# Four hand-overs of a four-layer convolution kernel: the first filter buffer, the last image's stores, layer 2's constants, layer 3's norms

## The chip, the cores and the metric

The kernel runs on one core of one Trainium2 chip, as one program and one launch. The metric is device time in microseconds (us). A core has five engines that run at the same time: TensorE (PE in the profile, its weight loads PEld), VectorE (DVE), ScalarE (ACT), GpSimd (POOL) and SyncE (SP). Each works through its own instructions in order. In this kernel nearly all DMAs are issued from SP's queue, so an SP issue that has to wait holds back every DMA behind it.

## The reference, cut to what matters

The input is 32 images of 96 channels of 56x56 values in float32. Four layers follow one another, each as `x = x + layer(groupnorm(x))`, the group norm in 32 groups of 3 channels:

```
x = x + L0(_gn(x))   # 1x1 96->576, BN, silu; depthwise 3x3, BN, silu; squeeze-excite; 1x1 576->96, BN; + identity
x = x + L1(_gn(x))   # depthwise 5x5 plus a three-level Haar wavelet transform with 5x5 depthwise filters on each level
x = x + L2(_gn(x))   # 4-bit quantised: 1x1 96->576, BN, clip, round; depthwise 3x3, ...; 1x1 576->96, BN; + identity
x = x + L3(_gn(x))   # depthwise 9x9 with a kernel computed from a 2x2 metric of each channel
```

In layer 2 a weight is quantised as `t = tanh(w); t = t / (2 max|t|) + 0.5; 2 round(15 t) / 15 - 1`.

## The kernel before, in words

**Layers 0 and 2** work image by image with channels on the partitions. An order written out by hand (`L0_ORDER`, `L2_ORDER`) fixes the sequence of steps on PE, DVE and ACT; `run_steps` walks it for image after image, with steps of the image before (`-`) and after (`+`) mixed in. In layer 0, `e` expands a block (PE, then ACT evicts into the padded buffer `hpad`, line 308), `f` makes a block's first depthwise tap on ACT (line 316), `t` makes one of the other eight taps on DVE (line 321), `a` and `c` make two further blocks' depthwise on PE (line 344), `p` projects (lines 402 to 405), `d` adds to the image (line 410) and `o` takes the image's statistics and stores it (line 417). The order begins:

```
    e00 e01 e02 e03 z0- f0 a3- z2- c1- e10 e11 t01 t02 g0- e12 t03 e30 e40 g1- s+ e13 t04 g2- g3-
    e31 e32 t05 e33 g4- t06 t07 u+ f1 m+ t11 p0- p1- q+ t08 d0- v+ w+ p2- t12 ...
```

**The tables.** Before layer 0's images, `tables()` makes the filters of layers 1 and 3 in the on-chip memory: `wavelet_filters` on DVE, with three buffers `zt` that POOL clears (line 485) and SP stores as `zwav` (line 497), and `diffusion_filters`, most of it on POOL (two `pow` at lines 1070 and 88, copies into `zdt`, line 1086), stored as `zdiff` (line 1087). All of it lies in one pool, `tables`, which is closed afterwards. The filter buffers `h2` of layer 0 (pool `l0h`, five of them) and the pool `l0l` are then opened where `tables` lay. From the stored filters SP builds matrices in DRAM (`twav`, `tdiff`) during layer 0.

**The end of layer 0.** When the last image is added, SP stores it in six DMAs, one for each group of 16 channels (`y0`, line 417). `store_norm` works out the scale and shift of layer 1's group norm for all channels and images (lines 106 to 119, with a `pow` on POOL at line 114) and SP stores the row (line 120) behind the image.

**Layer 1** works by pairs of channels, with rows of 14 image rows by phase on the partitions. For each pair, SP loads `X` (lines 538 and 541), `raw` and `T` matrices and `nr`, the row of norms (line 583), three pairs ahead; DVE normalises two pairs ahead (lines 654 and 655), ACT and DVE split `x` into two parts (`xh` line 662, `xl` line 666), and PE does the rest. The constants of layer 1 (`low1`, `up1`, `low2`, `up2`, line 604) are loaded first. After each pair, `behind` has SP load finished channel groups of `y1` into layer 2's first two image pairs (line 840).

**Layer 2's constants** are made by `Layer2.__init__` between layers 0 and 1: three weights are loaded (line 782) into a pool of their own, `l2t`, go through `tanh` on ACT (line 783), a largest value (DVE line 785, an all-reduce on POOL line 787) and rounding on DVE (lines 788 to 794); DVE then makes 45 diagonal matrices (line 808), and `folded` makes scales and offsets (lines 818 to 828).

**The end of layer 2** is like that of layer 0, but images are stored two at a time (line 1036). **Layer 3** works channel by channel: `load` first loads, for every eighth channel, the norms of eight channels (line 1107), then `X` and `raw`; ACT arranges `T`, DVE normalises (lines 1118 and 1119), PE filters (line 1126), DVE adds (line 1127), SP stores (line 1142).

Of the kernel before, what the change touches and what calls it, by code (L numbers as in the profile page):

```python
# [10 lines left out]
F32 = mybir.dt.float32  # L11
BF16 = mybir.dt.bfloat16
# [86 lines left out]
def store_norm(nc, S, pool, psum, mv, dram, bias):  # L99


    mc, d, dv, ve = (pool.tile([C, B], F32, tag=f"n{n}", name=f"n{n}", bufs=1) for n in ("mc", "d", "dv", "ve"))
    row = pool.tile([C, 2 * B + 1], F32, tag="row", name="row", bufs=1)
    rstd = row[:, 0:B]
    ps = psum.tile([128, 2, 512], F32, tag="mm", name="pn")
    nc.vector.tensor_copy(mc, mv[:, :, 0])
    nc.tensor.matmul(ps[:C, 0, :B], S.grp, mc, start=True, stop=True)
    nc.vector.tensor_tensor(d, mc, ps[:C, 0, :B], ALU.subtract)
    nc.vector.tensor_tensor(dv, d, d, ALU.mult)
    nc.vector.tensor_tensor(dv, dv, mv[:, :, 1], ALU.add)  # L110
    nc.vector.tensor_tensor(d, mc, d, ALU.subtract)
    nc.tensor.matmul(ps[:C, 1, :B], S.grp, dv, start=True, stop=True)
    nc.vector.tensor_scalar(ve, ps[:C, 1, :B], EPS_GN, None, ALU.add)
    nc.gpsimd.tensor_tensor(rstd, ve, S.mhalf[:C, :B], ALU.pow)
    nc.vector.scalar_tensor_tensor(row[:, B : 2 * B], d, -1.0, rstd, ALU.mult, ALU.mult)
    if bias is None:
        nc.vector.memset(row[:, 2 * B :], 0.0)
    else:
        nc.vector.tensor_copy(row[:, 2 * B :], bias)
    nc.sync.dma_start(dram, row)  # L120
# [24 lines left out]
def groups(t, y, at, store=False):  # L145

    for g in range(C // GR):
        part = t[g * GR : (g + 1) * GR], at(y[g])
        yield part[::-1] if store else part

# [13 lines left out]
def layer0(ctx, tc, S, x, w, y0, norm1, tables, aside):  # L164
# [66 lines left out]
    eye2 = cp.tile([128, HALF], F32, tag="eye2", name="eye2")  # L231
    nc.vector.tensor_tensor(eye2, S.ident[:, :HALF], S.ident[:, HALF:], ALU.add)
    diag = cp.tile([128, 2, 9, HALF], F32, tag="diag", name="diag")
# [3 lines left out]

    hpad = padded(cp, nc, 4, F32, "hpad")
    mv_all = cp.tile([C, B, 2], F32, tag="mv0", name="mv0")


    tables()
    hp = ctx.enter_context(tc.tile_pool(name="l0h", bufs=5))
    late = ctx.enter_context(tc.tile_pool(name="l0l", bufs=1))

# [68 lines left out]
    def first_tap(im, k):  # L314
        im["h2"][k] = hp.tile([128, H, W], F32, tag="h2", name="h2")
        nc.scalar.activation(im["h2"][k], window(im["pad"][k], 128, -1, -1, 0, H), AF.Copy,  # L316
                             scale=wdw[:, k, 0:1])
# [32 lines left out]
    def depthwise_ab(im, i):  # L350
        if i == 0:
            im["hab"] = late.tile([128, NP, 2, NT], F32, tag="hab", name="hab")
# [5 lines left out]
    def depthwise_c(im, i):  # L358

        if i == 0:  # L360
            im["hc"] = late.tile([128, 2, 2, NT], F32, tag="hc", name="hc")
# [28 lines left out]
    def gated(im):  # L390
        im["wg"] = late.tile([128, ND + 1, C], F32, tag="wg", name="wg")
# [15 lines left out]
    def add(im, i):  # L407
        for j in range(2):
            v = tiles(im["xt"])[:, i, j::2]
            nc.vector.scalar_tensor_tensor(  # L410
                v, im["ps"][i][:C, j, :NT].rearrange("c (x m) -> c m x", m=2), sc3, v, ALU.mult, ALU.add)

    def store(im):
        b, xt = im["b"], im["xt"]
        channel_stats(nc, sm, xt, mv_all[:, b, :], "t")
        for to, of in groups(xt, y0, lambda y: y[:, :, b, :], store=True):
            nc.sync.dma_start(to, of)
# [26 lines left out]
def wavelet_filters(nc, cp, w, z1, z2, z3):  # L444
# [15 lines left out]
    for v, z in enumerate((z1, z2, z3)):  # L460
# [23 lines left out]
        Z = cp.tile([C, 2, P, LEN, P, ks], F32, tag=f"z{v}", name=f"zt{v}")  # L484
# [12 lines left out]
        nc.sync.dma_start(z, Z.rearrange("c a p e o k -> c a p (e o k)"))  # L497

# [89 lines left out]
def layer1(ctx, tc, w, y0, norm, t1, t2, t3, y1, behind):  # L588
# [147 lines left out]
    with tc.manual_schedule(engines=MANUAL_SP):  # L736
        for i in range(-3, PAIRS):
# [25 lines left out]
            behind(2 * i + 2)  # L763


class Layer2:


    def __init__(self, ctx, tc, S, w, y1):
# [3 lines left out]
        self.pairs = [cp.tile([C, H * NPH, 2, W4], F32, tag=f"xt{i}", name=f"xt{i}") for i in range(2)]  # L773
        self.begun = 0

        CC, HALF, N9 = NBLK - 1, 64, 2 * NBLK - 1


        def quantized(name, shape, dtype):
            p, free = shape[0], shape[1:]  # L780
            t = tmp.tile(shape, F32, tag="t", name=f"{name}t")
            nc.sync.dma_start(t, w[name])
            nc.scalar.activation(t, t, AF.Tanh)
            m = cp.tile([p, 1], F32, tag=f"{name}m", name=f"{name}m")
            nc.vector.tensor_reduce(m, t, AX.X if len(free) == 1 else AX.XY, ALU.max, apply_absolute_value=True)
            a = cp.tile([p, 1], F32, tag=f"{name}a", name=f"{name}a")
            nc.gpsimd.partition_all_reduce(a, m, p, bass_isa.ReduceOp.max)
            nc.vector.tensor_scalar(a, a, 2.0, None, ALU.mult)
            nc.vector.reciprocal(a, a)
            nc.vector.tensor_scalar(t, t, a, 0.5, ALU.mult, ALU.add)  # L790
            nc.vector.tensor_scalar(t, t, 15.0, MAGIC, ALU.mult, ALU.add)
            nc.vector.tensor_scalar(t, t, MAGIC, 2.0, ALU.subtract, ALU.mult)
            o = cp.tile(shape, dtype, tag=f"{name}q", name=f"{name}q")
            nc.vector.tensor_scalar(o, t, 15.0, None, ALU.subtract)
            return o

        with tc.tile_pool(name="l2t", bufs=3) as tmp:
            w1 = quantized("l2_w1", [C, NBLK * 128], F32R)
            w2 = quantized("l2_w2", [128, NBLK, 9], F32)
            w3 = quantized("l2_w3", [128, N9 + 1, C], BF16)  # L800
        nc.vector.memset(w3[HALF:, N9 - 1, :], 0.0)
        nc.vector.memset(w3[:HALF, N9, :], 0.0)
        eye2 = cp.tile([128, HALF], F32, tag="eye2", name="eye2")
        nc.vector.tensor_tensor(eye2, S.ident[:, :HALF], S.ident[:, HALF:], ALU.add)
        diag = cp.tile([128, NBLK, 9, HALF], BF16, tag="diag2", name="diag2")
        for k in range(NBLK):
# [3 lines left out]
        mid = cp.tile([128, 10, N9], F32, tag="mid2", name="mid2")  # L810
        nc.sync.dma_start(mid, w["l2_mid"])
        out5 = cp.tile([C, 5, 1], F32, tag="out5", name="out5")
        nc.sync.dma_start(out5, w["l2_out"])
        def folded(a, p, n, tag, k, times):

            b_, g, be, m, v = (a[:, i, :] for i in range(5))
            s = cp.tile([p, n], F32, tag=f"s{tag}", name=f"s{tag}")
            nc.gpsimd.tensor_scalar(s, v, EPS_L2, None, ALU.add)
            nc.gpsimd.tensor_tensor(s, s, S.mhalf[:p, :n], ALU.pow)
            nc.vector.tensor_tensor(s, s, g, ALU.mult)  # L820
            o = cp.tile([p, n], F32, tag=f"o{tag}", name=f"o{tag}")
            nc.vector.tensor_tensor(o, b_, m, ALU.subtract)
            nc.vector.tensor_tensor(o, o, s, ALU.mult)
            nc.vector.tensor_tensor(o, o, be, ALU.add)
            if times != 1.0:
                nc.vector.tensor_scalar(o, o, times, None, ALU.mult)
            if k * times != 1.0:
                nc.vector.tensor_scalar(s, s, k * times, None, ALU.mult)
            return s, o

        s1, o1 = folded(mid[:, 0:5, :], 128, N9, "1", 1.0 / 15.0, 15.0)
        s2, o2 = folded(mid[:, 5:10, :], 128, N9, "2", 1.0 / 225.0, 15.0)
        s3, o3 = folded(out5, C, 1, "3", 1.0 / 225.0, 1.0)
        self.constants = w1, w3, diag, s1, o1, s2, o2, s3, o3

# [9 lines left out]
def layer2(ctx, tc, S, k2, y1, y2, norm3):  # L845
# [19 lines left out]
    pairs = k2.pairs + [cp.tile([C, H * NPH, 2, W4], F32, tag="xt2", name="xt2")]  # L865
# [158 lines left out]
    def add(im, i):  # L1024
        for j in range(2):
# [3 lines left out]
                v, im["ps"][i][:C, j, :NT].rearrange("c (r q) -> c r q", q=W4), s3, v, ALU.mult, ALU.add)  # L1029

    def store(im):
        b = im["b"]
        channel_stats(nc, sm, im["xt"], mv_all[:, b, :], "t")
        if b % 2:
# [15 lines left out]
def diffusion_filters(nc, cp, w, zd):  # L1050

# [22 lines left out]
    nc.gpsimd.tensor_tensor(kern, poi, kern, ALU.add)  # L1074
    rev = cp.tile([C, KS, KS], F32, tag="rev", name="rev")
    for ky in range(KS):
        nc.gpsimd.tensor_copy(rev[:, KS - 1 - ky], kern[:, KS * ky : KS * ky + KS])
    Z = cp.tile([C, NPH, LEN, NPH, NK], F32, tag="zd", name="zdt")
# [12 lines left out]
def layer3(ctx, tc, w, y2, norm, td, out):  # L1091
# [11 lines left out]
    def load(c):  # L1103
        if c % NN == 0:
            norms[c] = io.tile([128, NN, 2 * B + 1], F32, tag="nr", name="nr", bufs=3)
            rows = norm[c : c + NN].rearrange("c x -> (c x)").unsqueeze(0)
            nc.sync.dma_start(norms[c].rearrange("p c x -> p (c x)"), rows.to_broadcast([128, NN * (2 * B + 1)]))
        X = io.tile([128, 2, B, W4], F32, tag="X", name="X")
        load_halves(nc, X, y2[c // GR][c % GR])
        return {"X": X, "raw": load_matrices(nc, io, td, c), "nr": norms[c // NN * NN][:, c % NN]}  # L1110
# [18 lines left out]
    with tc.manual_schedule(engines=MANUAL_SP):  # L1129
        for c in range(-AHEAD, C):  # L1130
            if c + AHEAD < C:
                sts[c + AHEAD] = load(c + AHEAD)
            cur, far = sts.pop(c, None), sts.get(c + 2)
            if far:
                far["T"] = arranged(nc, io, far["raw"])
# [10 lines left out]
def kernel_body(tc, w, x, out):  # L1146
    nc = tc.nc
    with ExitStack() as ctx:
# [24 lines left out]
        def tables():  # L1173
            with tc.tile_pool(name="tables", bufs=1) as tp:
                wavelet_filters(nc, tp, w, z1, z2, z3)
                diffusion_filters(nc, tp, w, zd)
# [4 lines left out]
        with ExitStack() as ctx2:  # L1181
            k2 = Layer2(ctx2, tc, S, w, y1)

            layer1(tc, w, y0, norm1, t1, t2, t3, y1, lambda channels: k2.begin(min(channels - 2, C - GR)))
# [124 lines left out]
```

## Time and profile before

| | |
|---|---|
| median of 9 runs | 6487.06 us (6471.28 to 6495.83) |
| the profiled execution: its time, its span | 6489.56 us, 6487.6 us |
| instructions | 115298 |
| PE busy | 6023.1 us, 93% of the span |
| DVE busy | 5168.0 us, 80% |
| ACT busy | 3949.9 us, 61% |
| POOL busy | 206.9 us, 3% |
| mean granted TensorE clock | 0.966 |

The span runs from the first to the last instruction of one profiled execution; the time also has what lies around it, 2.0 us here. Rows of the timeline give start and duration in us, engine, line of the kernel, operation, output and inputs, the number of merged instructions and in brackets the idle time before and what ended it. A row of SPq is the issuing of DMAs, not their transfer.

In the page's 40 slices of 162 us, PE is busy for nine tenths or more of nearly every slice; the exceptions are the first slice, one at the change from layer 0 to layer 1, one at the change from layer 1 to layer 2, and one at the change from layer 2 to layer 3, besides the last.

### The profile page before, as it was taken

Reading aid. Unit: us, or ns where it says so; the run is one execution under the profiler, and the core shown is the slowest. Engines: PE = TensorE matmul, PEld = TensorE weight load, DVE = VectorE, ACT = ScalarE, POOL = GpSimd, SP = SyncE. Lnnn points to the kernel's source line nnn. Section 1 sums busy time; section 2 is a strip of 40 time slices with the busy share of each in tenths; the row PEclk is TensorE's granted clock in tenths of the full one; section 3 lists DMA queues with packets and bytes.
Section 4 is the critical chain, followed back from the end, with each engine's and each line's share of the span. In section 5 each row is a group of like instructions: output and inputs, shape, how many; then the busy total and the mean of one; then the engine's idle time right before and its main releaser. Section 6 shows DMA issues by size and latency. Waiting matters only on the chain. (4 is left out here: it accounts for less than half of the span.)

```text
span 6487.6 us, 115298 instructions
## 1 busy us (share of the span) xinstructions
PE 6023.1 (93%) x49064; PEld 3598.6 (55%) x49064; DVE 5168.0 (80%) x5468; ACT 3949.9 (61%) x5268; POOL 206.9 (3%) x158
## 2 busy tenths in 40 slices
PE   4999999999999999999949999989999999999699
PEld 2444444444444444444426555567777777778344
DVE  6999999998998998989946666657676767676577
ACT  4665666665765755656525555557676766677355
POOL 3000000000000000000010000000000000000000
PEclk7999999999999999999969999999999999999899
DMA  2162264528327264522535666656959595952688
GB/s 82 22 42 45 49 47 40 52 47 36 50 44 38 50 35 48 34 47 37 16 73 139 148 140 142 141 40 40 53 41 52 39 54 38 53 38 27 172 252 250
DMA packets 1609376, 452.91 MB, mean 70 GB/s; under 512 B 1425230, under 2 KB 1603142, under 8 KB 1605406
## 3 DMA queue, kind: packets, MB, share of 16 engines
q1 hardware_dynamic: 1608862, 445.54, 55.5%
q8 instruction: 385, 6.31, 0.5%
q14 instruction: 129, 1.06, 0.1%
HBM read 284.44 MB, written 214.08 MB: 77 GB/s over the span
## 5 line engine op out<-in xcount | busy, mean ns | idle before, releaser
L321 DVE SCALAR_TENSOR_TENSOR h<-hpad,l_wdw,h 128x3136 f32<-128x3136 f32 x768 | 2659.7, 3481 | 56.3 <-ACT h L316 42.3
L344 PE MATMUL psd<-hpad,diag 64*64 64x392 f32 x13824 | 1235.3, 511 | 3.3 <-issue 3.3
L308 ACT ACTIVATE hpad<-ps,o,s 128x784 f32<-128x784 f32 x640 | 684.3, 1080 | 774.4 <-PE ps L304 772.6
L304 PE MATMUL ps<-xn,l_wexp 96*128 96x392 f32 x2560 | 934.1, 517 | 103.0 <-ACT hpad L308 97.3
L984 PE MATMUL psd<-apad,diag 64*64 64x392 bf16 x20736 | 926.9, 332 | 110.3 <-issue 56.1
L344 PEld LDWEIGHTS psd<-hpad,diag 64*64 64x64 f32 x13824 | 528.6, 131 | 699.2 <-issue 660.4
L984 PEld LDWEIGHTS <-diag 64*64 64x64 bf16 x20736 | 712.1, 107 | 321.0 <-issue 161.1
L304 PEld LDWEIGHTS ps<-xn,l_wexp 96*128 96x128 f32 x2560 | 495.0, 198 | 492.6 <-ACT hpad L308 103.3
L955 ACT ACTIVATE u<-ps,o,s 128x784 int16<-128x784 f32 x576 | 536.4, 1002 | 160.5 <-PE ps L965 142.0
L955 ACT ACTIVATE a<-psd,o,s 128x784 int16<-128x784 f32 x448 | 426.8, 997 | 325.9 <-PE psd L984 324.5
L402 PE MATMUL psj<-h,wg 128*96 128x392 f32 x1536 | 589.0, 519 | 27.7 <-ACT hpad L308 26.1
L550 ACT COPY T<-raw 32x112 f32<-32x112 f32 (+2 forms) x1440 | 462.7, 384 | 242.9 <-DMA raw<-tdiff 211.2
L965 PE MATMUL ps<-hi,l_w1q 96*128 96x392 f32 x1280 | 461.5, 361 | 9.9 <-ACT hi L937 9.2
L1126 PE MATMUL pc<-x,T 128*112 128x416 f32 (+1 forms) x1152 | 415.7, 524 | 43.5 <-DMA X<-y 42.7
L721 PE MATMUL pc<-x,T 128*112 128x416 f32 (+1 forms) x1152 | 450.8, 528 | 0.0
L965 PE MATMUL ps<-lo,l_w1q 96*128 96x392 f32 x1280 | 436.8, 341 | 0.0
L402 PEld LDWEIGHTS psj<-h,wg 128*96 128x96 f32 x1536 | 248.8, 165 | 287.5 <-issue 255.9
L1126 PEld LDWEIGHTS pc<-x,T 128*112 128x112 f32 x1152 | 204.6, 178 | 254.0 <-issue 194.2
L327 ACT ACTIVATE hab<-psd,o,s 128x392 f32<-128x392 f32 x256 | 170.7, 671 | 262.3 <-PE psd L344 262.3
L316 ACT ACTIVATE h<-hpad,l_wdw 128x3136 f32<-128x3136 f32 x96 | 279.2, 2908 | 48.2 <-DMA zdiff<-zdt 47.1
L327 ACT ACTIVATE h<-h,o,s 128x3136 f32<-128x3136 f32 x96 | 287.9, 2999 | 18.6 <-DVE h L321 18.6
L721 PEld LDWEIGHTS pc<-x,T 128*112 128x112 f32 x1152 | 193.0, 180 | 146.6 <-issue 146.6
(207 smaller groups left out, 6766.1 us busy)
## 6 DMA issues: line engine op xcount, KB each, us to landing
X<-y SPq DMA_DIRECT2D x192, 392.0 KB
xt<-in_x_dram SPq DMA_DIRECT2D x32, 1176.0 KB
y<-xt SPq DMA_DIRECT2D x192, 196.0 KB
y<-y SPq DMA_DIRECT2D x96, 392.0 KB
xt<-y SPq DMA_DIRECT2D x96, 392.0 KB
y<-xt SPq DMA_DIRECT2D x96, 392.0 KB
out_dram<-y SPq DMA_DIRECT2D x96, 392.0 KB
twav<-zwav SPq DMA_DIRECT2D x768, 36.8 KB
```

The costliest lines, as they stand in the source:

```text
L304: nc.tensor.matmul(ps[:, j, :NT], wexp[:, k * 128 : k * 128 + 128], im["xn"][:, j, rows, :].rearrange("c h w -> c (h w)"), start=True, sto ...
L308: nc.scalar.activation(window(im["pad"][k], 128, 0, 0, 2 * i * RT, 2 * RT).rearrange("p r (w j) -> p j r w", j=2), ps[:, :, :NT].rearrange ...
L321: nc.vector.scalar_tensor_tensor(h2, window(im["pad"][k], 128, t // 3 - 1, t % 3 - 1, 0, H), wdw[:, k, t : t + 1], h2, ALU.mult, ALU.add,)
L327: nc.scalar.activation(view, ps, AF.Silu, bias=bi[1][:, c : c + 1], scale=sc[1][:, c : c + 1], accum_out=accum)
L344: nc.tensor.matmul(ps[c * HALF : (c + 1) * HALF, j, :NT].rearrange("p (r w) -> p r w", w=W2), diag[p, k - AB, t, :], v[:, :, j:W:2], start ...
L402: nc.tensor.matmul(out.rearrange("c (r w) -> c r w", w=W2), wg[:, k, :], im["h2"][k][:, rows, j::2], start=(k == 0), stop=False)
L550: nc.scalar.copy(to.rearrange("x t (p s) -> x t p s", p=NPH), v[:, k])
L721: nc.tensor.matmul(ps[:PH, to], st["T"][j][:, h, k, :], st["x"][:, j, h, of], start=False, stop=(n == NK - 1))
L955: nc.scalar.activation(out, ps, AF.Identity, bias=o[:, c : c + 1], scale=s[:, c : c + 1])
L965: nc.tensor.matmul(ps[:, j, :NT], w1[:, k * 128 : k * 128 + 128], im[part][:, r0 : r0 + RT, :].rearrange("c h w -> c (h w)"), start=(part ...
L984: nc.tensor.matmul(ps[q, j, :NT].rearrange("p (r w) -> p r w", w=W), diag[p, k, t, :], v, start=(t == 0), stop=(t == 8))
L1126: nc.tensor.matmul(ps[:, :, to], st["T"][:, h, k, :], st["x"][:, h, :, of], start=(n == 0), stop=(n == NK - 1))
```

## The change

Seven edits, in the order of the program:

- `h2s[0]`, the first of layer 0's five filter buffers, moves to the constants' pool `l0c`. The other four, and `hab`, `wg` and `hc`, become fixed tiles of one pool `l0l`, opened after `tables`.
- The tables are made in another order and in two pools: the diffusion kernel's values first, then the wavelet filters (the first buffer `zt0` and the small tiles in `tables`, the other two in `tables2`), then the diffusion filter, whose buffer is now the first half of `zt1`. Layer 0's `eye2` and `diag` come behind the tables in the program.
- The last image of layers 0 and 2 is stored tile by tile (24 DMAs in place of 6), each tile behind its own addition. In layer 2, image 30 is then stored alone.
- `store_norm` issues its store from ACT's queue.
- `Layer2.__init__` only lays out tiles. Loading, `tanh` with the largest value, rounding, `pow`, folding and five steps of nine diagonals become ten stages; `prepare` runs one of them behind each of the pairs 2 to 11 of layer 1. The raw weights lie in the second image pair's tile in the meantime.
- Loading channel groups for layer 2 begins when all stages are done.
- Layer 3 loads `X` and `raw` of four channels before the first norms.

```diff
-    nc.sync.dma_start(dram, row)
+    nc.scalar.dma_start(dram, row)
...
+def store_tile(nc, y, im, i):
+    rows = slice(i * 2 * RT * NPH, (i + 1) * 2 * RT * NPH)
+    for to, of in groups(im["xt"][:, rows], y, lambda y: y[:, rows, im["b"], :], store=True):
+        nc.sync.dma_start(to, of)
...
+    h2s = [cp.tile([128, H, W], F32, tag="h2", name="h2")]
+    tables()
     nc.vector.tensor_tensor(eye2, S.ident[:, :HALF], S.ident[:, HALF:], ALU.add)
...
-    hp = ctx.enter_context(tc.tile_pool(name="l0h", bufs=5))
     late = ctx.enter_context(tc.tile_pool(name="l0l", bufs=1))
+    h2s += [late.tile([128, H, W], F32, tag=f"h2{i}", name=f"h2{i}") for i in range(3)]
+    hab = late.tile([128, NP, 2, NT], F32, tag="hab", name="hab")
+    wg = late.tile([128, ND + 1, C], F32, tag="wg", name="wg")
+    h2s.append(late.tile([128, H, W], F32, tag="h23", name="h23"))
+    hc = late.tile([128, 2, 2, NT], F32, tag="hc", name="hc")
...
     def first_tap(im, k):
-        im["h2"][k] = hp.tile([128, H, W], F32, tag="h2", name="h2")
+        im["h2"][k] = h2s[(DV * im["b"] + k) % len(h2s)]
...
     def add(im, i):
...
+        if im["b"] == B - 1:
+            store_tile(nc, y0, im, i)
...
-        Z = cp.tile([C, 2, P, LEN, P, ks], F32, tag=f"z{v}", name=f"zt{v}")
+        Z = (cp2 if v else cp).tile([C, 2, P, LEN, P, ks], F32, tag=f"z{v}", name=f"zt{v}")
...
+        if v == 1:
+            room = Z[:, 0]
+    return room
...
-    Z = cp.tile([C, NPH, LEN, NPH, NK], F32, tag="zd", name="zdt")
+    Z = room
...
+        def largest():
+            for _, t, _, m, a in raw:
+                nc.scalar.activation(t, t, AF.Tanh)
+                nc.vector.tensor_reduce(m, t, AX.X, ALU.max, apply_absolute_value=True)
+                nc.gpsimd.partition_all_reduce(a, m, m.shape[0], bass_isa.ReduceOp.max)
...
+        self.stages = [load, largest, quantized, powers, folded] + [lambda k=k: diagonals(k) for k in range(NBLK)]
+
+    def prepare(self, pair):
+        if pair >= 2 and self.stages:
+            self.stages.pop(0)()
...
-            behind(2 * i + 2)
+            behind(i)
...
-        if b % 2:
+        if b == B - 2:
+            for to, of in groups(im["xt"], y2, lambda y: y[:, :, b, :], store=True):
+                nc.sync.dma_start(to, of)
+        elif b % 2 and b < B - 1:
...
     with tc.manual_schedule(engines=MANUAL_SP):
-        for c in range(-AHEAD, C):
-            if c + AHEAD < C:
-                sts[c + AHEAD] = load(c + AHEAD)
+        for c in range(AHEAD):
+            load(c)
+        load_norms(0)
+        for c in range(-2, C):
+            if 0 <= c < C - AHEAD:
+                load_norms(c + AHEAD)
+                load(c + AHEAD)
...
         def tables():
-            with tc.tile_pool(name="tables", bufs=1) as tp:
-                wavelet_filters(nc, tp, w, z1, z2, z3)
-                diffusion_filters(nc, tp, w, zd)
+            with tc.tile_pool(name="tables", bufs=1) as tp, tc.tile_pool(name="tables2", bufs=1) as tp2:
+                kernels = diffusion_kernels(nc, tp2, w)
+                room = wavelet_filters(nc, tp, tp2, w, z1, z2, z3)
+                diffusion_filters(nc, tp2, kernels, zd, room)
...
+            def behind(pair):
+                k2.prepare(pair)
+                if not k2.stages:
+                    k2.begin(min(2 * pair, C - GR))
```

## The prediction

> **What bounds the kernel now.** I read the page's slices first: PE is busy nine tenths or more everywhere but at the start and at the three changes of layer, so only time at those four places can go. Then the timeline of each place.
>
> The start (times in us from the span's start, then duration):
> ```profile
> 43.10 0.20 DVE L1067 TENSOR_SCALAR r<-r 96x81 f32<-96x81 f32 x1
> 43.22 13.30 POOL L1070 TENSOR_TENSOR kern<-two,arg 96x81 f32<-96x81 f32 x1 [21.54 <-DVE arg L1066]
> 57.16 13.32 POOL L88 TENSOR_TENSOR poi<-r,expoi 96x81 f32<-96x81 f32 x1
> 72.75 2.50 POOL L1086 COPY zdt<-rev 96x27 f32<-96x27 f32 x16
> 75.28 0.30 SPq L1087 DMA_DIRECT2D zdiff<-zdt  x1
> 81.21 2.91 ACT L316 ACTIVATE h<-hpad,l_wdw 128x3136 f32<-128x3136 f32 x1 [47.12 <-DMA zdiff<-zdt]
> 84.16 24.61 DVE L321 SCALAR_TENSOR_TENSOR h<-hpad,l_wdw,h 128x3136 f32<-128x3136 f32 x7 [40.85 <-ACT h L316]
> 108.75 6.87 DVE L321 SCALAR_TENSOR_TENSOR h<-hpad,l_wdw,h 128x3136 f32<-128x3136 f32 x2
> 115.77 3.75 POOL L277 TENSOR_TENSOR rstd<-ve,mhalf 96x1 f32<-96x1 f32 x1 [40.51 <-DVE ve L275]
> ...
> 4265.56 0.39 POOL L138 MEMSET apad<- 128x58 bf16 x4 [927.32 <-DMA y<-y]
> ```
> The first tap needs nothing of the tables, but its buffer lies in their memory: ACT, and behind it PE and DVE, stand until the last table is in DRAM. The last row shows that a pool waits for all pools that it lies over: the pad has nothing to do with `y`.
>
> Layer 0 to layer 1 (the fifth line is from the waits of SP's queue):
> ```profile
> 3277.66 1.15 DVE L410 SCALAR_TENSOR_TENSOR xt<-psj,sc,xt 96x392 f32<-96x392 f32 x2 [5.61 <-PE psj L405]
> 3278.88 27.35 SPq L417 DMA_DIRECT2D y<-xt  x6
> 3290.84 0.19 DVE L115 SCALAR_TENSOR_TENSOR row<-nd,row 96x32 f32<-96x32 f32 x1 [5.54 <-POOL row L114]
> 3306.67 4.58 SPq L120 DMA_DIRECT2D norm<-row  x1
> ...
> SPq L604 <- DVE l_w3q L794: 12.2, 1, 12.2
> ...
> 3339.61 0.87 SPq L583 DMA_DIRECT2D nr<-norm  x2
> 3345.44 0.90 DVE L654 TENSOR_TENSOR x<-X,nr 128x448 f32<-128x448 f32 x1
> 3354.60 0.74 PE L679 MATMUL pa<-xh,low1r 128*128 128x448 f32 x1 [69.53 <-DMA raw<-twav]
> ```
> The stores, then layer 2's constants, keep PE out. In layer 1 PE is full and DVE is not (busy PE, PEld, DVE ...):
> ```profile
> 3412.00:3430.00 18.00, 17.99 (x72) 10.95 (x71) 12.26 (x19) 10.77 (x29) 0.00 (x0) 1.00 0.48 141
> ```
> Layer 2 to layer 3:
> ```profile
> 6017.55 33.42 SPq L1036 DMA_DIRECT2D y<-xt  x6
> 6059.52 0.34 SPq L1107 DMA_DIRECT2D nr<-norm  x1
> 6059.91 0.42 SPq L538 DMA_DIRECT2D X<-y  x1
> 6066.50 28.91 PE L1126 MATMUL pc<-x,T 128*112 128x448 f32 x73 [42.73 <-DMA X<-y]
> ```
> From 6066.50 PE is busy 20.0 us of nearly every 20: layer 3 ends when PE's start lets it.
>
> **Step 1, the start.** The first tap's buffer is free: ACT makes `f0` when the fourth eviction is done, 34.1 to 37.0. DVE's table work ended at 43.3 and keeps its amount; the diagonals (6.2 us, before at 10.1 to 16.3) still find DVE waiting for the filters' loads (until 24.1). So taps start at 43.5, not 84.16. But the other buffers' pool lies over both table pools, so `f1` still waits for `zdiff`. The order has seven taps before `t11`, which reads `f1`: they end at 43.5 + 24.6 = 68.1. So POOL's end of the tables decides. Its first `pow` now comes at about 26.5 (loads 24.1, eight small DVE operations), the second ends at 26.5 + 27.3 = 53.8; then two small ones, 9 + 16 copies and the clearing (2.6, its first half of `zt1` stored by about 50, where the DMA's 300 GB/s fall off).
>
> Alone, that takes 7.1 us: `zdiff` issued at 61.1, landed 5.9 later (75.28 to 81.21), `f1` done at 69.9. But the taps now run beside it. POOL's `rstd` (line 277) takes 547 ns alone and 3630 in the median of layer 0, as long as a tap (3.48): it gets in between two taps only. At that price POOL does four small operations by 68.1 (boundaries at 57.4, 60.9, 64.4 and 67.9); then DVE stands, and the rest takes 0.95 + 2.6 + 2.5 = 6.1. `zdiff` is issued at 74.5, landed at 80.4, `f1` done at 83.4. `t11` moves from 108.75 to 83.4: **25.3 us**. From there the order is that of before, DVE 96 of 100 us busy. Bounds: 39 (alone) and 14 (the second `pow` held up too, below). I take 25, by the one row with POOL under taps.
>
> **Step 2, the last image of layer 0.** Six stores of 196 KB moved from 3280.2 to 3313.6, 33.4 us at 39 GB/s, and SP went on 2.1 us later. By tiles they begin behind the first addition (3258.5), 1.3 us later; a quarter takes 8.4 us and additions come every 6.8, so the queue never runs dry (SP waits at each tile for its addition, with only later tiles behind it): end 3259.8 + 33.4 = 3293.2, SP free at 3295.3. If 24 small DMAs cost 20% more, 6.7 later. The norm row is ready at 3291.0 and goes by ACT's queue; behind it on ACT are the `T` copies of layer 1, whose `raw` is not there yet. It lands well before it is read.
>
> **Step 3, layer 2's constants leave.** SP then issues layer 1's constants (1.8: 3332.93 to 3334.7), the first channel (3.65: 3317.0 to 3320.7), the second and the norms (5.7: 3334.8 to 3340.5), 11.2 together; `nr` lands 3.3 later. DVE normalises at 3309.8 where it did at 3345.44. Some of that will be lost to constants and `X` on the same engines: **34 us** for steps 2 and 3, bounds 27 and 37. The pipeline fills as before.
>
> What they cost in layer 1: one stage behind a pair. `tanh` is 2.0 us on ACT plus a table load, reductions 2.15 on DVE; rounding 5.0 on DVE (3328.3 to 3333.3); folding 17 x 0.15 = 2.6; nine diagonals 9 x 0.30 = 2.7. A pair leaves DVE 18.0 - 12.3 = 5.7 us idle, of which about 4.2 lie before the next `xl` that PE waits for: only rounding reaches past it, by 0.8. POOL's all-reduce and `pow` have a whole pair of time, SP's five issues (2.2 us) are three pairs ahead of need. **Minus 1**, bounds 0 and 6; with no cover at all, 2.15 + 5.0 + 2.6 + 13.5 = 23. The start of group loading moves from pair 8 to 11, for the first group only: nothing.
>
> **Step 4, layer 2 to 3.** Image 30 is added by 5980 and its store (33.4) keeps the DMA until about 6014.5. Image 31's tiles come at 6012.6 to 6017.6, too close to stagger, and end at 6014.5 + 33.4 = 6048; layer 3's memory is free at 6049.5, before 6059.5: 10 sooner. But now `nr` is issued behind four channels' loads, 3.3 us each on SP (6059.91 to 6063.19): at 6062.8, landing 3.3 to 4.8 later. DVE starts at 6066.1 to 6067.6, before at 6064.73. The ten are given back: **minus 2**, bounds minus 6 and plus 4.
>
> Sum: 25 + 34 - 1 - 2 = 56. The profiled execution of 6489.56 (span 6487.6) becomes 6433.6; the median, 2.5 lower, 6487.06 - 56 = 6431.
>
> **The rivals.**
> *POOL keeps its pace* (step 1 gives 39): 6487 - 70 = 6417. For: one-column `rstd` is a thin sample, and `pow` at 15.2 beside DVE's diagonals ran at its pace (1.34 us each). Against: those diagonals read one tensor, the taps two. 0.17.
> *The second `pow` and the taps meet.* It runs from 40.4 to 53.7, the taps start at 43.5. If the taps wait for its end, seven end at 78.3, POOL has 20 operations left (5.7 us), `f1` is done at about 93; if instead POOL gives way inside its `pow`, it has 8 to 9 us left at 68.1 and `f1` is done at 92.5. Either way 16 gained: 6440. For: nothing shows a long POOL operation under taps. Against: three taps around `rstd` took 10.51 where three take 10.45, so POOL held DVE up by 0.06 at most. 0.24. The Trainium skill (SBUF — State Buffer, Who interferes with whom) says that a DVE operation with two SBUF inputs and a GpSimd one that reads SBUF exclude each other for the whole instruction, whichever comes first; by that rule the taps would wait for the `pow`. The trace agrees on POOL's side (3630 ns) and not on DVE's (0.06).
> *Layer 1 has no room for the stages*: the 23 us are paid nearly in full, some 17 more than none: 6448. For: PE is 99.9% busy there. Against: DVE's 5.7 idle. 0.10.
> *Slower*: at pairs 2 to 11 each stage stops PE, since ACT or DVE, in order, waits for POOL or for the weights with the pair's work behind it. POOL's all-reduce once began 5.7 us late with no reason shown. It decides from 69 us, 6.9 in each of ten stages; at 8 it gives 6487 - 57 + 80 = 6510. Against: a pair of 18 us lies between asking and using. 0.05.
> *No difference*: the same at some 5 us a stage. 0.02.
>
> **How the numbers follow.** The forecast has 0.42: 6431, its own range 6423 to 6441. The range reaches over the first three rivals with their bounds: 6410 to 6458. Faster by over 0.2% (13 us, about what a measurement of this kernel can tell from no change) 0.93, within it 0.02, slower 0.05.
>
> **What would show it.** Right: the first tap on DVE near 43.5, seven taps, a gap of about 15 us before the eighth behind `f1`; `rev` and `zdt` copies stretched to a tap each; `nr` of layer 1 issued some 27 us behind layer 0's last addition (before 61); 18.0 us a pair through pairs 2 to 11; layer 3's first `nr` issue 13 us behind its first `X`. Wrong: `f1` not waiting for `zdiff`; the diagonals behind the tables' DVE work (6 us later taps); `X` of layer 3 issued before image 31 has landed (up to 8 sooner); a longer image in layer 0.

## The result, and the profile after

The changed kernel takes 6451.91 us (median of 9 runs, 6436.84 to 6465.57) where the kernel before takes 6486.05 beside it (29 runs, 6471.28 to 6504.68): 0.9948 of it, 95% interval 0.9938 to 0.9958, that is 34 us less (27 to 40). The forecast was 6431, 56 less. The profiled execution took 6445.33 us (span 6443.5). Measured between the same events in the two profiles:

| us | before | changed | gain | forecast |
|---|---|---|---|---|
| layer 0's `t11` begins | 108.75 | 83.25 | 25.5 | 25.3 |
| first image's statistics done | 220.4 | 197.7 | 22.7 | |
| last addition of layer 0 ends (E) | 3278.8 | 3258.8 | 20.0 | |
| from E to PE's first matmul of layer 1 | 75.8 | 47.0 | 28.8 | 34 |
| layer 1, first to last matmul | 907.2 | 910.7 | -3.5 | -1 |
| to the first matmul of layer 2 | 28.3 | 28.5 | -0.1 | 0 |
| layer 2, to its last addition | 1727.4 | 1719.9 | 7.5 | 0 |
| from there to layer 3's first matmul | 49.0 | 59.8 | -10.8 | -2 |
| layer 3, to the end | 421.1 | 418.9 | 2.2 | 0 |

The rows from E on, with the 20.0, make up the 44.1 us between the spans. Up to its last addition layer 2 computes the same in every kernel here and lasts from 1711 to 1741 us in their 14 profiles, so its 7.5 lies within what the same work varies by: without it 36.6 are left, near the 34 of the medians.

The start, from the timeline (start and duration in us):
```profile
41.00 13.32 POOL L88 TENSOR_TENSOR poi<-r,expoi 96x81 f32<-96x81 f32 x1
41.55 3.47 DVE L332 SCALAR_TENSOR_TENSOR h<-hpad,l_wdw,h 128x3136 f32<-128x3136 f32 x1
55.05 3.36 POOL L1116 TENSOR_TENSOR kern<-poi,kern 96x81 f32<-96x81 f32 x1
58.48 10.84 POOL L1125 COPY rev<-kern 96x9 f32<-96x9 f32 x9
69.25 2.61 POOL L1127 MEMSET zt<- 96x3024 f32 x1
71.93 2.50 POOL L1134 COPY zt<-rev 96x27 f32<-96x27 f32 x16
80.31 2.91 ACT L327 ACTIVATE h<-hpad,l_wdw 128x3136 f32<-128x3136 f32 x1 [31.77 <-DMA twav<-zwav]
83.25 6.88 DVE L332 SCALAR_TENSOR_TENSOR h<-hpad,l_wdw,h 128x3136 f32<-128x3136 f32 x2 [14.43 <-ACT h L327]
```
Taps begin at 41.6, the first two mixed with what is left of DVE's table work; then DVE stands for 14.4 us. The `pow` keeps its 13.32 us beside taps, and those keep their 3.47 to 3.51. The addition behind it (0.35 us alone) takes a tap's length, and the nine copies (1.20 alone) three taps. POOL's clearing and its 16 copies come when DVE stands, at their own pace. `f1`, the row at 80.31, waits for several DMAs at once; the last packets of `zdiff` end at 79.9, so it is the tables that it waits for, as forecast.

Layer 0 to 1, the timeline (the last addition ends at 3258.8):
```profile
3238.59 38.70 SPq L156 DMA_DIRECT2D y<-xt  x24
3282.75 0.36 SPq L621 DMA_DIRECT2D low<-in_low_dram  x1
3296.64 0.92 DVE L671 TENSOR_TENSOR x<-X,nr 128x448 f32<-128x448 f32 x1 [7.93 <-DMA nr<-norm]
```
SP goes on at E + 23.9, not at the forecast E + 16.6. In the waits of SP's queue there (us in total, times, longest) one row is new:
```profile
SPq L156 <- DMA norm<-row: 12.5, 1, 12.5
```
A tile store needs nothing of that row. The trace has eight semaphores (counters that tell an engine that something is done) for the landing of DMAs. In this program every DMA of SP and ACT takes the next of them in turn, and is not issued before the DMA that had it last has landed. The row's turn lay between the 18th and the 19th of the 24 tile stores, and ACT could issue it only at 3271.1, when POOL's `pow` was done.

What the stores themselves did is in three stretches (us, then busy PE, PEld, DVE, ACT, POOL, granted clock, DMA share, which passes 1 where packets overlap, GB/s): the six stores of the kernel before, then in the changed one the first 18 tile stores and the pause behind them.
```profile
3280.10:3312.50 32.40, 1.03 (x4) 0.79 (x4) 4.20 (x15) 0.00 (x0) 5.43 (x1) 0.54 0.40 38
3239.40:3263.50 24.10, 18.39 (x56) 8.60 (x55) 7.76 (x16) 0.00 (x0) 0.00 (x0) 0.99 1.07 38
3263.50:3273.40 9.90, 0.88 (x4) 0.61 (x4) 1.04 (x6) 0.00 (x0) 5.43 (x1) 0.50 0.01 3
```
Small stores were as fast as large ones, 38 GB/s, until the queue ran dry for 9.9 us. Had the last six followed at the pace of the 18 (8.0 us for six), they would have been done 7.8 us sooner and SP would have gone on at about E + 16: an estimate from these rows and the last packet, at 3279.3.

Layer 1, busy time in two stretches around the rounding stage (us, then PE, PEld, DVE, ACT, POOL, granted clock, DMA share, GB/s):
```profile
3407.12:3430.39 23.27, 23.26 (x92) 14.19 (x91) 18.65 (x40) 10.78 (x30) 0.00 (x0) 1.00 0.47 137
3430.39:3447.82 17.43, 14.21 (x51) 8.75 (x50) 12.17 (x18) 10.56 (x30) 0.00 (x0) 0.90 0.38 112
```
The stretches run from one `xl` of DVE to that of the next pair. One comes 5.25 us late, where a pair takes 18.02, and PE then has 3.2 us without work.

Layer 2 to 3:
```profile
5959.90 39.43 SPq L156 DMA_DIRECT2D y<-xt  x24
5963.70 1.15 DVE L1066 SCALAR_TENSOR_TENSOR xt<-psj,s,xt 96x392 f32<-96x392 f32 x2 [0.50 <-PE psj L1059]
6005.98 0.30 SPq L555 DMA_DIRECT2D X<-y  x1
6018.81 0.42 SPq L1156 DMA_DIRECT2D nr<-norm  x1
```
`nr` is issued 12.8 us behind the first `X`, as forecast; but the first `X` comes 41.1 us behind the last addition (before: 42.4, forecast: 32). SP waited 14.2 us for the norm row here, and the stores stood for 13.0 of them (2 GB/s from 5966.5 to 5979.5), between stretches in which they ran at 38 GB/s.

### The profile page after: what moved, and what is told of

It reads as the page before. It is cut to its first block, busy times and chain, and to the rows that moved or that the text cites. A ratio compares the mean times of both kernels' runs of the same rounds, so it can differ in the third digit from the quotient of the medians.

```text
span 6443.5 us, 115343 instructions
## 1 busy us (share of the span) xinstructions
PE 6026.5 (94%) x49064; PEld 3619.6 (56%) x49064; DVE 5168.3 (80%) x5468; ACT 3952.3 (61%) x5268; POOL 222.7 (3%) x158
## 4 chain that ended last, share of the span: by engine, by line
PE 73%; ACT 8%; DMA 5%; SPq 5%; DVE 4%; issue 3%; POOL 1%; POOLq 0%; ACTq 0%; DVEq 0%
PE psd L355 14%; PE psd L1022 10%; PE ps L315 9%; PE psj L413 8%; PE pc L1177 6%; PE ps L1003 6%; PE pc L738 5%; SPq L431 3%; PE psj L1059 3%; DMA y<-xt 3%; PE psj L415 3%; PE psj L416 3%; DVE h L332 2%; ACT hi L975 2%; ACT a L993 2%
## 5 line engine op out<-in xcount | busy, mean ns | idle before, releaser
L332 DVE SCALAR_TENSOR_TENSOR h<-hpad,l_wdw,h 128x3136 f32<-128x3136 f32 x768 | 2659.6, 3480 | 28.8 <-ACT h L327 14.8
L355 PEld LDWEIGHTS psd<-hpad,diag 64*64 64x64 f32 x13824 | 565.9, 132 | 660.8 <-issue 618.8
L1022 PEld LDWEIGHTS <-diag 64*64 64x64 bf16 x20736 | 693.5, 107 | 330.5 <-issue 155.2
## 6 DMA issues: line engine op xcount, KB each, us to landing
twav<-zwav SPq DMA_DIRECT2D x768, 36.8 KB
```

Of the source, the lines that this page charges most:

```text
L332: nc.vector.scalar_tensor_tensor(h2, window(im["pad"][k], 128, t // 3 - 1, t % 3 - 1, 0, H), wdw[:, k, t : t + 1], h2, ALU.mult, ALU.add,)
L355: nc.tensor.matmul(ps[c * HALF : (c + 1) * HALF, j, :NT].rearrange("p (r w) -> p r w", w=W2), diag[p, k - AB, t, :], v[:, :, j:W:2], start ...
L1022: nc.tensor.matmul(ps[q, j, :NT].rearrange("p (r w) -> p r w", w=W), diag[p, k, t, :], v, start=(t == 0), stop=(t == 8))
```

## The experiments

The kernel before took 6576 to 6587 us beside these runs, so ratios are compared, not times. They were made later and on three chips, where the same stores are slower: 32 to 34 GB/s between layers 0 and 1, in six or in 24, where both profiles above have 38. All ratios lie against the kernel before; the changed kernel, run again among them, had 0.9947 (0.9931 to 0.9963).

> The changed kernel itself, beside the next two kernels and on their chip: 0.9948 of the kernel before, as measured first; its parts as in its first profile: t11 at 82 to 84, PE's first matmul of layer 1 47 to 49 us behind layer 0's last addition, layer 1 908 to 912 us, PE's first matmul of layer 3 60 to 66 us behind layer 2's last addition.

Measured there: `t11` at 82.0, PE's first matmul of layer 1 at E + 48.9, layer 1 910.7 us, layer 3's first matmul 63.5 us behind layer 2's last addition. These are the numbers that the experiments stand beside.

**The norm row on SP**
```diff
-    nc.scalar.dma_start(dram, row)
+    nc.sync.dma_start(dram, row)
```


> The changed kernel with one edit undone: both norm rows are stored from SP's queue again, behind the tile stores. In the changed kernel's profile SP's tile stores wait 12.5 us (layer 0 to 1) and 14.2 us (layer 2 to 3) for the norm row, a DMA of another queue. Theory A, the row on ACT's queue takes a turn between the tile stores and a later store has to wait for that turn: without it the 24 stores run through. SP goes on about 14 us behind layer 0's last addition E (changed kernel: E + 24) and 31 us behind layer 2's (changed: E + 41); 18 to 20 us sooner in all, some 6433 us for 6452. Theory B, 24 small stores simply take 20% longer than 6 large ones (38.7 and 39.4 us for 33.4): nothing is gained, the row's issue on SP adds 1 to 4 us, 6453 to 6456.

0.9955 (0.9943 to 0.9967). The wait for the row is gone, and next to nothing is won:
```profile
3370.86 0.36 SPq L621 DMA_DIRECT2D low<-in_low_dram  x1
```
The last addition ends at 3348.8. SP goes on at E + 22.1 (25.0 in changed_again), and at layer 2's end at 43.8 (45.1). In changed_again SP's waits for the row were 9.9 and 7.8 us, and taking them away won 2.9 and 1.3. Theory A's size fell, but theory B is not shown by it: the 24 stores, now without a gap, run at 32 GB/s, and six large ones run at 34 in undo_tiles. With slower stores more is still queued when the wait begins, so that changed_again's stores stand for only 6.6 and 4.2 us, where those of the first changed profile stood for 9.9 and 13.0. What the wait costs where stores run at 38 GB/s no run shows.

**Six stores for the last image again**

The edit takes `store_tile` out of both `add` functions and stores the last image of layer 0, and the last pair of layer 2, in six.

> The changed kernel with the last image of layer 0 stored in six DMAs behind its last addition, and the last two images of layer 2 together in six, both as before; the row stays on ACT's queue. Behind the last addition E of layer 0, SP went on at E + 36.8 in the kernel before and E + 23.9 in the changed one; behind that of layer 2 at E + 42.4 and E + 41.1 (E + 43.8 to 47.5 in the four kernels run since). Theory A, small stores are about as fast as large ones and start earlier: both hand-overs are 12 us longer here, 24 us slower than changed. Theory B, 24 small stores are slower byte for byte (27 to 32 GB/s where six large ones have 36 to 39), and image 30 stored alone doubles the packets of the last two images: layer 0 to 1 is 11 to 13 us longer, layer 2 to 3 is up to 5 us shorter, 8 to 12 us slower in all.

0.9969 (0.9951 to 0.9986), some 14 us slower than the changed kernel. SP goes on at E + 42.2 behind layer 0, 17 later than with tiles; PE's first matmul of layer 1 comes at E + 66.4. Behind layer 2 it is 43.6 against 45.1: there the tiles bring nothing. So neither theory's size was right, and B's was nearer, but not for its reason: the six run at 34 GB/s, hardly faster than the tiles of changed_again ahead of their pause (33). The tiles pay in layer 0, whose additions lie 6.8 us apart. In layer 2 the additions are close together and the store of image 30 alone lies ahead (see pair_tiles).

**Layer 2's constants between the layers again**

The edit brings back `Layer2.__init__` and `behind(2 * i + 2)`.

> The changed kernel with layer 2's constants made between layers 0 and 1 as before (and group loading from pair 8). Tiles stores and the row's queue stay as changed. Theory A, the constants cost the hand-over what lay between SP's going on and DVE's first norm: before, DVE normalised 28.4 us behind the first X on SP, in the changed kernel 12.0; so PE's first matmul comes about 16 us later behind layer 0's last addition (E + 63 for E + 47), and the stages' 3.5 us within layer 1 are won back (pair of 23.3 us back to 18): 12 to 13 us slower, 6464. Theory B, stages in layer 1 cost nothing and the 3.5 us are chance: 16 slower, and the same long pair in another place.

0.9972 (0.9960 to 0.9983), some 16 us slower than the changed kernel. One row of SP's waits shows what the constants do:
```profile
SPq L621 <- DVE l_w3q L811: 16.4, 1, 16.4
```
SP has issued the first `X` at E + 26.2, but layer 1's constants wait for DVE's rounding, and PE begins at E + 70.6. With tiles alone PE is thus 5.2 us sooner than before (75.8), with the constants alone (undo_tiles) 9.4, with both 27 to 29: each of the two hid most of what the other is worth. Layer 1 takes 904.2 us (907.2 in the kernel before); the eight profiles with all ten stages take 907.8 to 911.6, on average 910.0. The stages cost 3 to 6 us. Both terms of theory A are there, and both are larger than it said.

**Rounding in three stages**
```diff
-            for _, t, o, _, a in raw:
+            for _, t, o, _, a in raw[i : i + 1]:
...
+        self.stages = [load, largest, *(lambda i=i: quantized(i) for i in range(3)), powers, folded]
```


> The changed kernel with the rounding stage split into three stages, one weight each (twelve stages behind pairs 2 to 13 in place of ten). Theory A, the rounding's 6.4 us of DVE work in one pair reach past DVE's idle time of that pair, and PE loses 3.2 us behind it (14.2 us busy of 17.4 in the changed profile): split, no pair between 2 and 13 loses more than 0.5 us, layer 1 is 3 us shorter (907.5 us from PE's first matmul to its last, 910.7 in the changed profile). Theory B, PE loses there for another reason, as DVE waiting for POOL's all-reduce: the loss stays in one of the pairs.

0.9947 (0.9934 to 0.9959). The long pair of 23.3 us is gone: the pairs with the three stages take 18.5, 17.3, 19.9 and 16.2, 71.9 together, which is what four pairs take elsewhere (18.02 each), and PE has no gap in them. Theory A. Layer 1 takes 905.6 us here and 907.3 to 908.7 in the three later kernels with this edit, for 910.0 on average: the 3.2 us of PE's gap, less than the ratio can tell.

**The start as before**

> The changed kernel with the first filter buffer, the order of the tables and their two pools as before. Theory A, the prediction's step 1 as the changed profile shows it: layer 0's t11 goes back from 83.3 to about 108.8 (25.5 us), and nothing else moves: 6476 to 6478 us. Theory B, part of the start's gain is given back inside the first image (114.5 us from t11 to its statistics in the changed kernel, 111.6 before): then the first image has 111.6 us here, and the kernel is 22 to 23 us slower than the changed one, 6475.

0.9998 (0.9986 to 1.0009), about 0.005 above the changed kernel (33 us, give or take 13). `t11` is at 107.9 and the first image's statistics come 111.6 us later, at 219.5; in the seven other kernels with the changed start and filter work among these runs they come at 194.7 to 198.0, on average 195.8. So 25 us are won at `t11` and 23.7 are left an image later: theory B. In the first image of the changed kernel DVE waits twice for PE (2.2 and 2.1 us in the first profile, 2.2 and 0.9 in changed_again), which it does not here.

**POOL's work for the filter cut down**
```diff
-    nc.vector.tensor_tensor(r2, z[:, 0], z[:, 1], ALU.add)
+    for ky in range(KS):
+        to, of = (slice(KS * y, KS * y + KS) for y in (ky, KS - 1 - ky))
+        nc.vector.tensor_tensor(r2[:, to], z[:, 0, of], z[:, 1, of], ALU.add)
...
-    rev = cp.tile([C, KS, KS], F32, tag="rev", name="rev")
-    for ky in range(KS):
-        nc.gpsimd.tensor_copy(rev[:, KS - 1 - ky], kern[:, KS * ky : KS * ky + KS])
+    rev = kern.rearrange("c (y x) -> c y x", x=KS)
...
-            nc.gpsimd.tensor_copy(Z[:, pi, lo : lo + KS, po, valid[0] : valid[-1] + 1], rev[:, :, kx::NPH])
+            nc.scalar.copy(Z[:, pi, lo : lo + KS, po, valid[0] : valid[-1] + 1], rev[:, :, kx::NPH])
```


> The changed kernel with POOL's work for the diffusion filter cut down: the rows are flipped by DVE when it adds the two squares (nine small additions in place of one, so POOL's nine rev copies are gone), and the 16 copies into the filter's buffer are made by ACT, which stands idle there. In the changed profile POOL's last addition of the kernel's values took 3.36 us and the nine copies 10.84 us under the taps (0.35 and 1.20 alone), and f1 comes at 80.3, t11 at 83.3. Theory A, small POOL operations with reads are held until a tap ends, and nothing else: the clearing (2.6) runs freely, ACT's copies too (3 to 4 us): t11 at 74 to 75, 8.5 us sooner. Theory B, the clearing is held as well: t11 at 77 to 79. Theory C, ACT's copies are held too: no gain.

0.9930 (0.9918 to 0.9943).
```profile
41.14 16.72 POOL L88 TENSOR_TENSOR poi<-r,expoi 96x81 f32<-96x81 f32 x1
41.18 3.47 DVE L332 SCALAR_TENSOR_TENSOR h<-hpad,l_wdw,h 128x3136 f32<-128x3136 f32 x1
58.45 3.30 POOL L1118 TENSOR_TENSOR kern<-poi,kern 96x81 f32<-96x81 f32 x1
61.70 2.61 POOL L1127 MEMSET zt<- 96x3024 f32 x1
64.34 2.10 ACT L1134 COPY zt<-kern 96x27 f32<-96x27 f32 x16 [15.54 <-POOL zt L1127]
75.35 6.88 DVE L332 SCALAR_TENSOR_TENSOR h<-hpad,l_wdw,h 128x3136 f32<-128x3136 f32 x2 [6.70 <-ACT h L327]
```
`t11` comes at 75.4 (82.0 in changed_again), theory A. The clearing runs under taps in its own 2.61 us, ACT's copies too. The Trainium skill (SBUF — State Buffer, Who interferes with whom) says that a DVE operation with two SBUF inputs contends with a GpSimd one that reads SBUF and not with one that only writes it; the addition (3.30) and the clearing (2.61) agree. But the `pow` also reads, and here it took 16.72 us: it began 0.04 us before a tap, a whole tap longer than in the changed kernel, where it began 0.55 before. The three later kernels with this edit repeat both numbers (16.71 to 16.72, 0.04); the other eight with the changed start have 13.32 to 13.37, begun 0.51 to 0.55 before. That a POOL operation is held only while it fetches or stores, and not while it computes, fits both; it was not tried alone.

**Layer 3's norms first again**
```diff
+        load_norms(0)
         for c in range(AHEAD):
             load(c)
-        load_norms(0)
```


> The changed kernel with one edit undone: layer 3 loads its first norms ahead of the four channels again. In the changed kernel nr is issued 12.8 us behind the first X, and DVE waits for it until 17.1 us behind the first X. Theory A, nr is what layer 3's start waits for, and the norm row landed 26 us before: nr issued first is there 3.3 to 4.8 us later, DVE starts 5 us behind the first X and PE 6.5 behind it (18.6 in the changed kernel): 11 to 12 us sooner, about 6441 us. Theory B, the loads of the next channels are then what PE waits for (3.3 us a channel on SP, 3.6 on PE, and the T copies of ACT behind them): layer 3 is up to 3 us longer after its first matmul, so 8 to 9 us sooner.

0.9937 (0.9922 to 0.9951). PE's first matmul comes 6.8 us behind the first `X` (18.4 in changed_again) and 52.1 behind layer 2's last addition (63.5); layer 3 then takes 420.7 us from its first matmul to the last instruction of PE or DVE, against 414.8 to 419.3 in the nine profiles with the changed order (415.9 to 420.6 in the three later kernels with norms first): 11.4 us won and on average some 2 given back, within what layer 3 varies by. Theory A is shown, theory B's loss is not told from chance.

**Tile stores from two queues, alone and with the other edits**
```diff
-        nc.sync.dma_start(to, of)
+        (nc.scalar if g % 2 else nc.sync).dma_start(to, of)
```


> The changed kernel with every second of the 24 tile stores issued from ACT's queue in place of SP's; the norm row behind them on ACT's. Theory A, what limits the stores is the issuing queue (SP is busy 34.5 to 42 us with issuing 24 of them, the share of the DMA engines was 0.4 with six large stores): with two queues the rate nearly doubles, SP goes on 10 to 14 us behind layer 0's last addition (24 now) and 15 to 20 us behind layer 2's (41 to 47 now), 25 us or more faster than changed. Theory B, the DMA engines or the memory behind them are the limit (share 0.7 to 0.95 with tile stores): the same bytes take the same time, SP goes on within 3 us of where it does now.

0.9931 (0.9918 to 0.9945). SP goes on at E + 21.0 (25.0; 22.1 in row_on_sp, with one queue and no wait): theory B. Behind layer 2 it is 36.8 (45.1), but not by the queues: image 31 took longer in this profile, so that image 30's stores began 44.0 us ahead of the last addition (38.5 in changed_again). From first to last packet the two images' stores took 76.1 us, against 77.3 in row_on_sp and 79.3 in changed_again. Then four edits together:

> The changed kernel with four edits together that were each run alone: the flipped kernel with ACT's copies (t11 at 75.4 for 83.3), the rounding in three stages (layer 1 4 us shorter), layer 3's norms first (PE's first matmul 6.8 us behind the first X for 18 to 19, of which some 3 us are given back in layer 3), and the tile stores from two queues (SP 3 us sooner behind layer 0, 8 us sooner behind layer 2). Theory A, they lie in different places and add: 8 + 4 + 8 + 11 = 31 us faster than changed, 0.990 of the kernel before; PE's first matmul of layer 3 at 44 to 46 us behind layer 2's last addition. Theory B, two queues and norms first get in each other's way, since the norm row goes by ACT's queue behind ACT's tile stores and nr now waits for it first: layer 3's first matmul stays at 50 to 55, 22 to 25 us faster.

0.9913 (0.9895 to 0.9931). PE begins layer 1 at E + 45.4 and layer 3 at 51.2, as theory B had it, but not for its reason. The first `X` comes at 44.4 again because image 30's stores begin 37.7 us ahead of the last addition, as in most of the profiles, and not 44.0; the two images' stores take 77.7 us. So the 8 us that the expectation took from two_queues behind layer 2 were luck of one profile.

> The same as four_edits, but the last image of layer 0, and the last two images of layer 2 together, stored in six DMAs behind the last addition, alternately from SP's and ACT's queue. Six from SP alone took 33.4 us with the DMA engines busy four tenths. Theory A, the issuing queue is the limit for large stores: six from two queues take 17 to 20 us, SP goes on some 22 us behind layer 0's last addition (21 with tiles from two queues) and 22 behind layer 2's (37): 15 us faster than four_edits. Theory B, memory takes packets of 56 and 112 bytes no faster: 33 us again, SP goes on at 37 to 42 behind both, 16 to 20 us lost between layers 0 and 1, nothing won between 2 and 3.

0.9947 (0.9927 to 0.9967), theory B:
```profile
3348.14 16.60 SPq L428 DMA_DIRECT2D y<-xt  x3
3348.16 22.80 ACTq L428 DMA_DIRECT2D y<-xt  x3
3389.89 0.36 SPq L618 DMA_DIRECT2D low<-in_low_dram  x1
```
SP goes on 41.8 us behind layer 0's last addition (3348.1) and 43.7 behind layer 2's, with one queue (undo_tiles) 42.2 and 43.6. The Trainium skill (DMA: Bandwidth & Descriptors, Issuing engines are not separate DMA queues) says that DMAs of all engines run on the same 16 DMA engines, and that several issuers only save issuing time; the run agrees.

**Image 30 and 31 together, by tiles**
```diff
-            store_tile(nc, y2, im, i)
+            store_tile(nc, y2, im["pair"], slice(B - 2, B), i)
```


> The same as four_edits, but images 30 and 31 of layer 2 are stored together, tile by tile (24 stores of 98 KB, runs of 112 bytes), in place of image 30 alone in six and image 31 in 24 (runs of 56 bytes). Theory A, stores of so short runs are priced by the packet, not by the byte: 21504 packets took 33.4 us in the kernel before both for an image alone (1.2 MB) and for a pair (2.4 MB), so image 30 stored alone adds 21504 packets right ahead of image 31's: with the pair the queue is empty at the first tile, SP goes on 33 to 37 us behind layer 2's last addition (44.4 in four_edits), PE's first matmul of layer 3 comes at 40 to 44 (51.2): 8 us faster than four_edits, 0.990 of the kernel before. Theory B, priced by the byte: 2.4 MB in tiles take 70 us or more, SP goes on at 60 or later, 15 us slower.

0.9903 (0.9882 to 0.9925), the lowest ratio of all, though not told from four_edits: 64 us less than the kernel before (49 to 78). The 24 stores of layer 0's last image (56 bytes a packet), the 24 of layer 2's last two (112 bytes), and SP's going on (the last addition ends at 6052.3):
```profile
3320.00:3358.80 38.80, 19.21 (x58) 9.20 (x56) 8.79 (x22) 0.00 (x0) 5.43 (x1) 0.80 1.63 32
6048.20:6085.60 37.40, 3.89 (x22) 2.64 (x20) 8.38 (x22) 0.00 (x0) 5.43 (x1) 0.57 1.53 65
6089.15 0.34 SPq L1154 DMA_DIRECT2D nr<-norm  x1
```
Twice the bytes in the same number of packets take the same time, and the memory of layer 3 is free 7 us sooner: `X` at 37.3 behind the last addition, PE at 44.0. Such stores are priced mostly by the packet, and image 30 alone had added 21504 of them. In six stores twice the bytes cost somewhat more: the pair's packets took 40.1 us in the kernel before, layer 0's last image 32.4. (The 33.4 us that the expectation gives for the pair is the row of its issue.)

## Why the prediction was right or wrong

The sign was right and the time lies in the stated range (6410 to 6458), but the size was not right: 56 forecast, 34 measured. 6451.91 lies outside the forecast's own 6423 to 6441; the range reached it for the sake of rivals that fell, so that part is luck. At the measured events step 1 is 5 us short at the end of layer 0, steps 2 and 3 another 5, the stages 2.5 and step 4 some 9. By its own steps:

- **Step 1** held to 0.2 us at `t11`, and its reason held: POOL's end of the tables decides, and small POOL operations wait for the end of a tap. Two of its details were wrong and cancelled. Not one operation gets in at each end of a tap but three (nine copies in three taps), so no copy into `rev` was left when DVE stood; but DVE stood 0.7 us later, since its table work lay between the first taps. The copies into the filter were not stretched, as they came after the taps. That the stall in the first image takes 1 to 3 us back was not in it; the rest, from 22.7 to 20.0 at the end of layer 0, lies in later images and is no more than ACT's waits for their loads vary by (57.4 us before, 60.9 changed). (Its lower bound, 14, is not what its rival works out to, 16.)
- **"POOL keeps its pace"** fell with the 10.84 us of the copies. **"The second `pow` and the taps meet"** fell in the changed profile (13.32 us), though flip_act shows that half a microsecond decides whether a tap's length is added.
- **Steps 2 and 3** were mis-sized: 34 forecast, 28.8 measured. SP went on at E + 23.9 (16.6 forecast). The prediction sent the norm row by ACT's queue and gave it no price, as it lands long before it is read; but the row takes its turn among the semaphores of all DMAs, and SP's stores wait for that. The stores themselves ran as forecast (8.0 us for a tile, 8.4 forecast), so the 6.7 us that it kept for smaller DMAs were not needed, and the estimate of 7.8 us for the pause covers the 7.3 that SP was late. That price is not shown by a run: row_on_sp won 2.9 us, where stores are slower. The chain behind SP held: DVE normalised 13.9 us after SP went on (14.5 forecast).
- **Step 3's price in layer 1**, 1 forecast, 3.5 measured. The rounding took DVE 7.1 us, not 5.0 (the doubling and the reciprocal of each largest value lie ahead of the stretch from which the 5.0 were taken, and done one weight after the other the steps overlap less), and the cover was 1.9, not 4.2: the next pair's normalising, which `xl` needs, was due that early. "Layer 1 has no room" stays far off: its 17 more were not there, nor the stalls of "slower".
- **Step 4** was the largest miss, 2 forecast and 10.8 measured, and the same wait is in it: image 31's tiles were to be done 30.5 us behind the last addition, and were done at 38.3 with 13.0 us of pause. The 13 us from the first `X` to `nr` were right, but were to be paid out of 10 us that never came. norms_first shows that this order alone costs 11 us at layer 3's first matmul, pair_tiles that storing image 30 alone costs 7 where stores are slower.
- **"Only time at those four places can go"** was not right either: a slice of 162 us at nine tenths hides stalls of 10 us. Seven images of layer 0 are together 78 us longer than seven of the others in the kernel before (last section). In its layer 1 PE waits 17.7 us in five places, each behind a late `nr`:
```profile
DVE x L654 <- DMA nr<-norm: 43.1, 5, 9.1
```
Each of the five ends 25 to 27 us after SP began to load a channel group for layer 2 (line 840). The changed kernel has five such waits too. Whether other places for these loads would save them was not tried.

## What to carry to other kernels

- Stores of short runs cost mostly by the packet: 21504 packets took 32 to 39 us with 56 bytes each and 37 to 40 with 112, in six DMAs or in 24, from one queue or from two. To split such a transfer pays only where its pieces are ready far earlier than the whole, and to take a transfer out of a shared one adds its packets again.
- A wait that a change brings is not yet its price: look at what is still queued behind it, and take it away (9.9 us of wait and 2.9 of price in changed_again). The price need not be the same where the transfers run at another pace.
- A DMA moved to another queue can still hold up the queue that it left. Look for a wait that names a DMA with no data in common.
- Of two edits at one hand-over, each may be worth little alone and the pair much: judge them by removing each from the whole, not by adding each to nothing.

## What the runs showed of the hardware that was not expected

Every third to fifth image of layer 0 takes 106 to 110 us where the others take 96.3 to 98.2. The prediction put layer 0 down to PE and DVE; the waits of ACT in one such image of the changed profile name a load:
```profile
ACT junk L273 <- DMA xt<-in_x_dram: 9.8, 1, 9.8
```
In changed_again the same image takes 124.5 us, and the same row reads 16.6. There layer 0 from its first image's statistics to its last addition takes 3146 us against 3061, with the DMA engines busy 0.63 of the time for the same 40 GB/s (0.47), while layers 1 and 2 take what they took. So layer 0 makes up 85 of the 95 us between the two spans, all of it in the same seven images. ACT's waits for their loads are 127.6 us there against 60.9, so that most of it is these waits. The experiments' times lie 1.4% higher, for the kernel before too, of which there is no profile there. Which DMAs hold those loads back, and whether an earlier load would win the 10 us in seven images, was not tried.
